# A recommender forward pass with word rows gathered by three engines: instructions recorded with the kernel's own semaphores, and more columns fetched row by row

## The chip, the cores and the metric

The kernel runs on one core of a Trainium2 chip. The metric is the device time in microseconds of one execution, as the median of several. The trace is that of one profiled execution, and its span goes from the core's first instruction to its last.

The engines are TensorE (PE, with PEld for its weight loads), VectorE (DVE), ScalarE (ACT), GpSimd (POOL) and SyncE (SP). A name with q (SPq, ACTq) is an engine's sequencer, which issues DMAs.

## The reference

For each of 16384 rows, 32 word indices pick rows of 300 floats out of a table of 50000, and their mean is taken. Three groups of 20 indices and four single ones do the same with small tables of 64 columns, each with one more column for the "wide" sum. The 748 features go through three layers with ReLU and a last one with a sigmoid.

```python
tok = word_emb[token_idx].mean(axis=1)          # (16384, 300) from 32 rows each
e1 = emb_mh1[mh1_idx].mean(axis=1)              # tables of 1000, 5000, 10000 rows
...
o4 = emb_oh4[oh4_idx]                           # tables of 100, 50, 20, 1000 rows
emb = jnp.concatenate([tok, e1, e2, e3, o1, o2, o3, o4], axis=1)
wide = (wide_mh1[mh1_idx].sum(axis=(1, 2)) + ... + wide_oh4[oh4_idx][:, 0])[:, None]
h = jax.nn.relu(emb @ W1 + b1)                  # 748 -> 1024
h = jax.nn.relu(h @ W2 + b2)                    # -> 512
h = jax.nn.relu(h @ W3 + b3)                    # -> 256
return jax.nn.sigmoid(h @ Wd + bd + wide)
```

## The kernel before

The rows are worked in 128 tiles of 128. A tile has 11 steps (`STEPS`), and the main loop runs over `n_steps` = 128 x 11 + 27 = 1435 steps. In one step the program writes the instructions of several pieces of work, each by its own pace:

- Words. `tokens` goes over the 32 word columns of a tile in 16 groups of two. One indirect DMA on POOL gathers 128 rows of 300 floats (one column) into `tok_rows`, which has six buffers of two columns. Three groups later (`TOK_LAG`) `add_up` adds them on DVE into `own`, a PSUM bank; the last add of a tile goes into the features `g`.
- Some columns come another way. `fetch` lets SP read column 31 of a tile row by row: `load_column` loads the 128 indices into one partition (`columns`), `column_offsets` turns them into byte offsets with two operations on DVE, and for each 32 rows a TENSOR_LOAD reads 32 offsets into registers, and 32 DMAs of 1200 bytes follow, each behind a MOVE of the register, into one of two buffers `fetched`. A column is spread over 16.5 steps (`FETCH_STEPS`), and those of 83 tiles (from tile 4, all with t % 3 not 0) go this way. `ScalarRows` lets ACT read column 30 of 26 tiles likewise, 8 offsets per TENSOR_LOAD, into `fetched_scalar`. ACT's rows go out wherever the running number of transfers reaches one of two places of eight, so one for each three of SP's.
- Small tables. `one_hots` compares indices with an iota on DVE (`hot`), ACT scales half of it, `counts` multiplies one-hot matrices on PE into `pc`, and ACT evicts these counts as `cnt` in FP8. `small_sums` multiplies `cnt` with the tables' terms into `pg` on PE, and DVE reduces that into `g`.
- The layers run on blocks of 3, 2 or 1 tiles, on PE with ACT's eviction, some matmuls in each step.

Order and waits: PE, DVE, ACT and SP execute in the order in which the program is written (`manual_schedule`), and the framework sets the waits from the tile pools. Every hardware transfer takes one of eight semaphores in turn (the lanes DMAHW0 to 7, six of them for SP and two for ACT while ACT's rows run) and waits for the lane's last transfer; each gather does the same with the lanes DMASW0 to 7. Where an instruction has more waits than fit, an event instruction of its own stands ahead of it.

Of the kernel before, what the change touches and what calls it, by code (L numbers as in the profile page):

```python
# [14 lines left out]
U8 = mybir.dt.uint8  # L15
AF = mybir.ActivationFunctionType
# [13 lines left out]
FETCH_STEPS = 16.5  # L30
FETCH_AHEAD = {1: 25.0, 2: 19.5}
# [4 lines left out]
SCALAR_LANES = (6, 7)  # L36
SCALAR_FROM = 12
SCALAR_RATE = 2.55
SCALAR_MARGIN = 5.0
SCALAR_LOADS = 8  # L40
SCALAR_WANTED, SCALAR_LEAST = 8, 2
# [41 lines left out]

@with_exitstack
def kernel(
# [24 lines left out]
    M1, M2, M3 = D1 // P, D2 // P, D3 // P  # L110

# [8 lines left out]
    tokp = ctx.enter_context(tc.tile_pool(name="tok", bufs=TOK_BUFS))  # L120
    const = ctx.enter_context(tc.tile_pool(name="const", bufs=1))
    idxp = ctx.enter_context(tc.tile_pool(name="idx", bufs=4))
    keyp = ctx.enter_context(tc.tile_pool(name="keys", bufs=1))
    scp = ctx.enter_context(tc.tile_pool(name="sc", bufs=2))
    ohp = ctx.enter_context(tc.tile_pool(name="onehot", bufs=HOT_BUFS))
    cp = ctx.enter_context(tc.tile_pool(name="counts", bufs=2))
    fp = ctx.enter_context(tc.tile_pool(name="fetched", bufs=2))
    fa = ctx.enter_context(tc.tile_pool(name="fetched_scalar", bufs=2))
    gp = ctx.enter_context(tc.tile_pool(name="g", bufs=3))
    wp = ctx.enter_context(tc.tile_pool(name="wide", bufs=2))  # L130
    xp = ctx.enter_context(tc.tile_pool(name="x", bufs=1))
    hp = ctx.enter_context(tc.tile_pool(name="h", bufs=1))
    ps_h = ctx.enter_context(tc.tile_pool(name="ps_h", bufs=2, space=bass.MemoryType.PSUM))
    ps_c = ctx.enter_context(tc.tile_pool(name="ps_c", bufs=2, space=bass.MemoryType.PSUM))
    ps_g = ctx.enter_context(tc.tile_pool(name="ps_g", bufs=1, space=bass.MemoryType.PSUM))
    ps_v = ctx.enter_context(tc.tile_pool(name="ps_v", bufs=1, space=bass.MemoryType.PSUM))

# [13 lines left out]
    NK = len(chunk_rows)  # L151
    N_EARLY = 3

    transfers = []
    scalar_row = []

    def hardware_dma(queue, **operands):

        dma = queue.dma_start(**operands)  # L161
        if transfers and transfers[-1][0] is not queue:
            tc.add_manual_dep(
                dma.ins,
                transfers[-1][1],
                mybir.DependencyInfo(mybir.DependencyClass.NoSync, mybir.DependencyReason.DATA),
                reason="the semaphores of transfers are taken in this order",
            )
        transfers.append((queue, dma.ins.name))

    def sync_dma(**operands):

        while len(transfers) % LANES in SCALAR_LANES and scalar_row and scalar_row[0]():
            pass
        hardware_dma(nc.sync, **operands)

    ident = const.tile([P, P], F32, name="ident")
    make_identity(nc, ident)
    ident_bf = const.tile([P, P], BF16, name="ident_bf")
# [3 lines left out]
    scale = const.tile([P, NK], F32, name="scale")  # L183
# [11 lines left out]
    own = ps_v.tile([P, 512], F32, name="own")  # L195
    tok_sum = own[:, 128 : 128 + TOK_D]
    iota_i = keyp.tile([P, n_h], I32, name="iota_i", tag="low")
    nc.gpsimd.iota(iota_i, pattern=[[1, n_h]], base=0, channel_multiplier=0)
    iota_s = keyp.tile([P, n_h], BF16, name="iota_s", tag="keys")
# [4 lines left out]
    first = const.tile([P, 1, N_SMALL], I32, name="first")  # L204
# [6 lines left out]
    terms = const.tile([P, n_h, 3 * ROW], BF16, name="terms")  # L211
    early_use = fa.tile([P, TOK_D], F32, name="fetched_scalar")
# [6 lines left out]
    def load_tables(part0, tag):  # L219
        raw = hp.tile([P, PART, ROW], F32, name="raw", tag=tag)  # L220
# [12 lines left out]
        return raw  # L233

    def convert_tables():
# [19 lines left out]
        def make(p, c):  # L255
# [5 lines left out]
            left = ps_h.tile([P, SPLIT, ROW], F32, name="left", tag="ph")[:, 0 : b - a, :]  # L261
# [13 lines left out]
    w1_sb = const.tile([P, NK, D1], F32, name="w1_sb")  # L275
    w2_sb = const.tile([P, M1, D2], F32, name="w2_sb")
    w3_sb = const.tile([P, M2, D3], F32, name="w3_sb")
    wd_sb = const.tile([P, M3], F32, name="wd_sb")
    b1_sb = const.tile([P, M1], F32, name="b1_sb")
    b2_sb = const.tile([P, M2], F32, name="b2_sb")  # L280
    b3_sb = const.tile([P, M3], F32, name="b3_sb")
    bd_sb = const.tile([1, 1], F32, name="bd_sb")
# [14 lines left out]
    def features(t):  # L297
        if t not in g_of:
            g_of[t] = gp.tile([P, G_COLS], F32, name="g")
# [21 lines left out]
    def tokens():  # L321

        under_way = []
        for n in range(n_all):
            if n < n_all - TOK_LAG:
                t, q = divmod(n, n_groups)
                it = token_indices[t // NSUB][:, t % NSUB, :].bitcast(U32)
                tok_rows = tokp.tile([P, TOK_GROUP * TOK_D], F32, name="tok_rows")
                rows = []
                for r in range(TOK_GROUP):  # L330
                    j = q * TOK_GROUP + r
                    if (t, j) in fetched:
                        rows.insert(0, fetched.pop((t, j)))
                        continue
                    assert j != N_TOK - 2 or t not in asked_tiles
                    rows.append(tok_rows[:, r * TOK_D : (r + 1) * TOK_D])
                    gather = nc.gpsimd.indirect_dma_start(  # L337
                        out=rows[-1],
                        out_offset=None,
                        in_=word,  # L340
                        in_offset=bass.IndirectOffsetOnAxis(ap=it[:, j : j + 1], axis=0),
                    )
                    tc.stamp_issue_order_token(gather.ins, "gathers")
# [5 lines left out]
    fetched, columns, asked_tiles = {}, {}, set()  # L349
    all_columns = const.tile([P, P], I32, name="columns")  # L350
    uses = {True: 0, False: 0}
    word_bytes = word.bitcast(U8).rearrange("n d -> (n d)").unsqueeze(0)

    def load_column(t, j, by_scalar):
# [4 lines left out]
        operands = dict(out=columns[t, j], in_=idx[t * P : (t + 1) * P, j : j + 1].rearrange("n o -> o n"))  # L359
        if by_scalar:  # L360
            hardware_dma(nc.scalar, **operands)
        else:
            sync_dma(**operands)
# [9 lines left out]
    def load_offsets(column, p0, n, engine):  # L373

        _, values = nc.values_load_multi_w_load_instructions(
            column[:, p0 : p0 + n],
            engines=[engine],
            min_val=0,
            max_val=(word.shape[0] - 1) * ROW_BYTES,
            skip_runtime_bounds_check_because="the indices are rows of the table",  # L380
        )
        return values

    def fetch(t):


        rows = fp.tile([P, TOK_D], F32, name="fetched").bitcast(U8)
        column = columns.pop((t, N_TOK - 1))
        for p0 in range(0, P, LOADS):
            for i, value in enumerate(load_offsets(column, p0, LOADS, mybir.EngineType.SP)):  # L390
                p = p0 + i
                sync_dma(out=rows[p : p + 1, :], in_=word_bytes[:, bass.ds(value, ROW_BYTES)])
                if p == P - 1:
                    fetched[t, N_TOK - 1] = rows.bitcast(F32)
                yield 1

    class ScalarRows:
# [3 lines left out]
        def __init__(self, summed_at, column_due):  # L401
            self.summed_at, self.column_due = summed_at, column_due
            self.step, self.t, self.next_t = 0, None, None
            self.row, self.values, self.loaded, self.issued = P, [], P, 0
            self.ready, self.starts, self.asked = set(), [], True

        def choose(self, rows_before):

            least = self.step + (rows_before + P) / SCALAR_RATE + SCALAR_MARGIN
            t = next((t for t in range(tiles_all) if self.summed_at(t) >= least), None)  # L410
            if t is None or t > tiles_all - 3:
                return None
            return t

        def load(self, free):

            if len(self.values) >= (SCALAR_WANTED if free else SCALAR_LEAST):
                return
            if self.loaded == P:
                if self.next_t not in self.ready:  # L420
                    return
                self.starts.append(self.next_t)
                self.column, self.loaded = columns.pop((self.next_t, N_TOK - 2)), 0
                self.next_t = None
            self.values += load_offsets(self.column, self.loaded, SCALAR_LOADS, mybir.EngineType.Activation)
            self.loaded += SCALAR_LOADS

        def __call__(self):

# [567 lines left out]
```

## Time and profile before

| | |
|---|---|
| median of three runs | 7411.62 us |
| lowest and highest | 7397.10, 7412.59 us |
| span of the profiled execution | 5019.3 us |
| own time of the profiled execution | not given; the median stands 2392.3 us above the span |
| granted TensorE clock, mean | 0.990 |
| busy in the span: PE, PEld, DVE, ACT, POOL | 4806.3, 3721.3, 3748.7, 2726.5, 3774.2 us |
| gathers on POOL | 3987, 946 ns each |
| row DMAs on SP, on ACT | 10624, 3328 |

The profile counts an instruction of an engine as busy from its start to its end. DMA-issuing instructions are not counted as busy on SP and ACT, so these queues have to be read from the lists by tile and from the timeline, where `fetched` is SP's rows and `fetched_scalar` ACT's. The time outside the span is in no view of the profile.

### The profile page before, as it was taken

The page shows a single profiled execution, that of the slowest core. Times are in us where ns is not written, and L with a number is a line of the kernel's source. Part 1 is how long each engine was busy: PE and PEld are TensorE (multiplying, and loading weights), DVE is VectorE, ACT ScalarE, POOL GpSimd, SP SyncE. Part 2 cuts the span into 40 slices and gives each one's busy share as a digit, 9 for nine tenths or more (in the row PEclk, how much of TensorE's full clock was granted, in tenths as well). Part 3 has the DMA queues.
Part 4 walks back from the last instruction along what each step waited for, and adds up shares of the span by engine and source line. Part 5 has one row for each costly group of instructions (what it writes and reads, how often), then busy time and mean ns, then how long its engine had stood idle before and what let it go on. Part 6 is the DMA issues. An engine that isn't in the chain of part 4 may idle for free.

```text
span 5019.3 us, 124363 instructions
## 1 busy us (share of the span) xinstructions
PE 4806.3 (96%) x36356; PEld 3721.3 (74%) x36356; DVE 3748.7 (75%) x6830; ACT 2726.5 (54%) x3658; POOL 3774.2 (75%) x3994
## 2 busy tenths in 40 slices
PE   6799999999999999999999999999999999999999
PEld 4577777777777777777777777667767888888899
DVE  6777777777777777777777777777777777777774
ACT  5455555555555555555555555555555555555552
POOL 7777777777777777777777777777777777777775
PEclk8899999999999999999999999999999999999999
DMA  7444444444444444444444444444444444444443
GB/s 204 127 129 130 129 129 129 129 130 129 129 130 128 129 130 129 130 129 129 129 129 129 130 129 129 130 129 129 130 130 129 129 129 130 130 129 130 129 128 100
DMA packets 291735, 654.13 MB, mean 130 GB/s; under 512 B 147100, under 2 KB 161692, under 8 KB 291048
## 3 DMA queue, kind: packets, MB, share of 16 engines
q0 software_dynamic: 191376, 612.66, 45.1%
q1 hardware_dynamic: 89271, 29.49, 2.7%
q10 hardware_dynamic: 10400, 4.02, 0.4%
q8 instruction: 284, 4.65, 0.4%
q14 instruction: 404, 3.30, 0.2%
HBM read 645.65 MB, written 0.07 MB: 129 GB/s over the span
## 4 chain that ended last, share of the span: by engine, by line
PE 37%; DMA 26%; DVE 15%; issue 12%; POOL 9%; ACT 1%; SPq 1%; ACTq 0%; DVEq 0%; POOLq 0%
DMA tok_rows<-in_word_emb_dram,it 23%; PE ph L677 17%; PE pg L554 14%; POOL tok_rows L337 9%; DVE hot L501 5%; DVE own L319 4%; PE pc L519 4%; DVE own L314 3%; DMA fetched_scalar<-in_word_emb_dram 1%; DMA fetched<-in_word_emb_dram 1%; PE pc L595 1%; DVE g L544 1%; PE po L719 1%; SPq L161 1%; DVE x L599 0%
## 5 line engine op out<-in xcount | busy, mean ns | idle before, releaser
L337 POOL DMA_INDIRECT tok_rows<-in_word_emb_dram,it x3987 | 3773.3, 946 | 1219.3 <-issue 754.1
L508 ACT ACTIVATE hot<-hot 64x768 bf16<-64x768 bf16 (+1 forms) x1408 | 1155.4, 821 | 1820.6 <-DVE hot L501 1664.0
L554 PE MATMUL pg<-terms,cnt 128*128 128x195 bf16 x17664 | 1723.7, 249 | 35.6 <-DVE g L544 35.0
L554 PEld LDWEIGHTS <-cnt 128*128 128x128 fp8e3 x17664 | 1529.2, 98 | 83.1 <-issue 54.4
L677 PE MATMUL ph<-x,w_sb 128*128 128x384 f32 (+5 forms) x4932 | 1473.8, 437 | 16.2 <-ACT h L688 11.9
L501 DVE TENSOR_TENSOR hot<-own,sc 128x1656 bf16<-128x1656 bf16 (+1 forms) x1408 | 1393.7, 990 | 126.7 <-PE pc L519 37.7
L522 ACT ACTIVATE cnt<-pc 128x828 uint16<-128x828 f32 (+1 forms) x1408 | 1186.5, 843 | 181.5 <-PE pc L519 103.2
L319 DVE TENSOR_TENSOR own<-own,tok_rows 128x300 f32<-128x300 f32 x1792 | 857.1, 478 | 513.3 <-DMA tok_rows<-in_word_emb_dram,it 468.5
L677 PE MATMUL ph<-h,w_sb 128*128 128x384 f32 (+2 forms) x4160 | 1225.9, 435 | 14.2 <-ACT h L688 14.0
L314 DVE TENSOR_TENSOR own<-own,tok_rows 128x300 f32<-128x300 f32 x1827 | 873.8, 478 | 271.9 <-DMA tok_rows<-in_word_emb_dram,it 221.0
L677 PEld LDWEIGHTS ph<-x,w_sb 128*128 128x128 f32 (+1 forms) x4932 | 830.8, 191 | 305.7 <-ACT h L688 23.0
L519 PEld LDWEIGHTS <-hot 128*128 128x128 bf16 x8192 | 594.2, 98 | 523.8 <-issue 271.3
L677 PEld LDWEIGHTS ph<-h,w_sb 128*128 128x128 f32 x4160 | 700.6, 191 | 266.1 <-ACT h L688 27.3
L519 PE MATMUL pc<-hot 128*128 128x138 bf16 x8192 | 733.1, 225 | 111.8 <-ACT hot L508 51.7
L688 ACT ACTIVATE h<-ph,b_sb 128x384 f32<-128x384 f32 (+2 forms) x723 | 378.7, 524 | 210.5 <-PE ph L677 115.4
L544 DVE TENSOR_REDUCE g<-pg 128x130 f32<-128x390 f32 (+1 forms) x512 | 259.2, 506 | 140.0 <-PE pg L554 138.7
L599 DVE TENSOR_TENSOR x<-pc,scale 128x768 f32<-128x768 f32 x127 | 120.8, 951 | 58.8 <-PE pc L595 57.5
L595 PE MATMUL pc<-ident,g 128*128 128x128 f32 x762 | 107.3, 278 | 5.7 <-ACT cnt L522 5.4
L312 DVE TENSOR_TENSOR own<-tok_rows 128x300 f32<-128x300 f32 x128 | 61.5, 481 | 55.3 <-DMA tok_rows<-in_word_emb_dram,it 52.6
L595 PEld LDWEIGHTS pc<-ident,g 128*128 128x128 f32 x762 | 83.7, 143 | 9.8 <-ACT cnt L522 9.3
L488 DVE COPY sc<-pc 128x512 bf16<-128x512 bf16 x64 | 44.0, 688 | 40.5 <-PE pc L484 39.8
L719 PE MATMUL po<-h,wd_sb 128*1 128x384 f32 (+2 forms) x208 | 67.4, 442 | 4.4 <-ACT h L688 4.4
(59 smaller groups left out, 514.6 us busy)
## 6 DMA issues: line engine op xcount, KB each, us to landing
fetched<-in_word_emb_dram SPq DMA_DIRECT2D x10624, 1.2 KB
tok_rows<-in_word_emb_dram,it POOLq DMA_INDIRECT x3987
fetched_scalar<-in_word_emb_dram ACTq DMA_DIRECT2D x3328, 1.2 KB
ix<-in_idx_dram SPq DMA_DIRECT2D x64, 64.0 KB
w_sb<-in_W_dram SPq DMA_DIRECT2D x6, 512.0 KB
raw<-in_mh_dram SPq DMA_DIRECT2D x4, 682.5 KB
it<-in_idx_dram SPq DMA_DIRECT2D x64, 32.0 KB
w_sb<-in_W_dram SPq DMA_DIRECT2D x1, 2048.0 KB
```

The lines of the kernel that those rows point to most:

```text
L314: nc.vector.tensor_add(tok_sum, tok_sum, a)
L319: nc.vector.tensor_add(to, tok_sum, b)
L337: gather = nc.gpsimd.indirect_dma_start(out=rows[-1], out_offset=None, in_=word, in_offset=bass.IndirectOffsetOnAxis(ap=it[:, j : j + 1], ...
L501: nc.vector.tensor_tensor(hot[:, 0 : 2 * rows, :].rearrange("p i (n d) -> p i n d", d=2), iota.rearrange("p (n d) -> p n d", d=2).unsqueez ...
L508: nc.scalar.activation(upper, upper, AF.Copy, scale=UPPER)
L519: nc.tensor.matmul(pc[:, k // n, at : at + n_h], hot[:, 2 * k, 0:P], hot[:, 2 * k + 1, :], start=True, stop=True)
L522: nc.scalar.activation(cnt[:, :, b : b + rows].rearrange("l h (g k) -> l h g k", g=2), pc[:, :, 0 : n * n_h].rearrange("l g (k h) -> l h g ...
L544: nc.vector.tensor_reduce(field_columns(features(t), pair), pg[:, 0:n, :].rearrange("p f (c d) -> p f d c", c=3), AX.X, ALU.add,)
L554: nc.tensor.matmul(pg[:, j, :], by_slice[:, h, :], terms[:, h, :], start=(h == h0), stop=(h == h1 - 1))
L595: nc.tensor.transpose(pt[:, j // n, j % n, :], g[:, c : c + P], ident)
L677: nc.tensor.matmul(to, weights[: src.shape[0], k, m * P : (m + 1) * P], src, start=(k == 0), stop=(k == len(srcs) - 1),)
L688: nc.scalar.activation(dst()[:, m, 0:n], ph[:, 0:n], AF.Relu, bias=bias[:, m : m + 1])
```

## The change

The framework's pools, schedule and waits are replaced by classes of the kernel's own. `Queue` and `Program.record` record each instruction with the regions that it reads and writes; from these follow its waits, without those that another wait already implies. `Program.emit` writes all recorded instructions at the end, in one critical section, in the recorded order on each engine, with the kernel's own semaphores: one for each engine that is waited for, eight lanes for other transfers, one for each of the six `tok_rows` buffers, and eight in turn for SP's columns and for ACT's. `Ring` and `Banks` are fixed buffers in place of pools.

A batch is the gathers of one `tok_rows` buffer, or the 128 rows of a column. Whoever reads one waits for its last member, and its members wait for nothing of their own:

```diff
+    def record(self, emit, sequencer, stream, reads, writes, clear=(), batch=None):
+        ins = Instruction(emit, sequencer, self.stream(stream))
+        if batch is not None:
+            batch.append(ins)
+            ins.batch = batch
+        needed = {}
+        def need(other):
+            other = other.batch[-1]
+            if other.batch is ins.batch:
+                return
...
+        waits = [o for s, o in needed.items() if known.get(s, 0) < o.tick]
+        waits = [
+            o
+            for o in waits
+            if not any(d is not o and d.knows(o.stream) >= o.tick for d in waits)
+        ]
...
-                    gather = nc.gpsimd.indirect_dma_start(
...
-                    tc.stamp_issue_order_token(gather.ins, "gathers")
+                    program.gather(f"gather{tokp.slot}", rows[-1], word, it[:, j : j + 1], batch, tok_rows)
```

The row fetches are planned anew. `RowFetches` sets column behind column from a first step, `FETCH_STEPS` or 128 / `SCALAR_RATE` steps each, and picks for each the next tile whose sum is wanted at least `FETCH_MARGIN` steps after its end. SP's first column starts at step 31 and its last ends at step 1423; DVE prepares a column's offsets one step before its rows start. ACT's rows no longer hang on the lanes: three are issued in each step ahead of `one_hots`, two behind it.

```diff
-FETCH_STEPS = 16.5
-FETCH_AHEAD = {1: 25.0, 2: 19.5}
+FETCH_STEPS = 14.5
+FETCH_MARGIN = 3.0
...
-SCALAR_LANES = (6, 7)
-SCALAR_FROM = 12
-SCALAR_RATE = 2.55
+ROW_SEMAPHORES = 8
+SCALAR_FROM = 8
+SCALAR_BEFORE, SCALAR_AFTER = 3, 2
+SCALAR_RATE = SCALAR_BEFORE + SCALAR_AFTER
...
+            by_sync.prepare(step)
+            by_scalar.prepare(step)
+            scalar_rows(step, SCALAR_BEFORE)
             if i < STEPS - 1:
                 hot = one_hots(sc, s, i + 1)
...
-            fetch_rows(step, 0.5)
+            scalar_rows(step, SCALAR_AFTER)
+            sync_rows.to(step + 0.5)
             flush_outputs()
             counts(cnt, hot_now, i)
-            fetch_rows(step, 1)
+            sync_rows.to(step + 1)
```

| in the program | before | after |
|---|---|---|
| columns fetched by SP, by ACT | 83, 26 | 96, 52 |
| row DMAs on SP, on ACT | 10624, 3328 | 12288, 6656 |
| TENSOR_LOADs on SP, on ACT | 332, 416 | 384, 832 |
| gathers on POOL | 3987 | 3948 |
| event instructions, all engines | 8164 | 3100 |
| of them on DVE, POOL, ACT, SP | 5487, 2032, 92, 529 | 1889, 52, 1096, 52 |

On PE the instructions and their order stay; of its waits before, 2171 stood on weight loads and 1579 on matmuls, and of the 2424 after, all stand on weight loads.

SP before, in the middle of a column: each row is one instruction with the wait for its lane, here with the block's indices (`it`, `ix`) between.

```order
L161 DMA fetched<-in_word_emb_dram 1x1200 [waits DMAHW0_49]
L161 DMA fetched<-in_word_emb_dram 1x1200 [waits DMAHW1_49]
L375 TENSOR_LOAD columns [waits DVE_49]
L161 DMA fetched<-in_word_emb_dram 1x1200 [waits DMAHW2_49,DVE_49]
L161 DMA fetched<-in_word_emb_dram 1x1200 [waits DMAHW3_49]
L161 DMA fetched<-in_word_emb_dram 1x1200 [waits DMAHW4_49]
L161 DMA fetched<-in_word_emb_dram 1x1200 [waits DMAHW5_49]
L161 DMA it<-in_idx_dram 128x2x32 [waits DMASW5_49,DMASW4_49,DMASW6_49,DMASW3_49,DMASW7_49,DMASW2_49,DMAHW0_49,DMASW1_49,DMASW0_49]
```

SP after, from the last rows of one column (`fetched_80`) into the next: rows without waits stand as one line with their count.

```order
L259 TENSOR_LOAD columns
L238 DMA fetched_80<-in_word_emb_dram 1x1200 x32
L259 TENSOR_LOAD columns [waits sem_DVE]
L238 DMA fetched_81<-in_word_emb_dram 1x1200 x32
L259 TENSOR_LOAD columns
L238 DMA fetched_81<-in_word_emb_dram 1x1200 x32
L259 TENSOR_LOAD columns
L238 DMA fetched_81<-in_word_emb_dram 1x1200 x19
L232 DMA out_dram<-x 3x1x128 [waits sem_ACT]
```

A column's rows have no wait any more; its first load of offsets waits for DVE's two operations, and the store of results, which stands between rows, for ACT.

ACT before, in the steady part: one or two rows between its ACTIVATEs, each with its lane.

```order
L161 DMA fetched_scalar<-in_word_emb_dram 1x1200 [waits DMAHW7_49]
L522 ACTIVATE cnt<-pc 128x138x6 [waits PE_49]
L508 ACTIVATE hot<-hot 64x6x128 [waits DVE_49]
L688 ACTIVATE h_39476<-ph,b_sb 128x384 [waits PE_49]
L522 ACTIVATE cnt<-pc 128x138x6 [waits PE_49]
L161 DMA fetched_scalar<-in_word_emb_dram 1x1200 [waits DMAHW6_49]
```

ACT after, in the same part: three rows ahead of the scaling of `hot`, two behind it.

```order
L238 DMA fetched_scalar_82<-in_word_emb_dram 1x1200 x3
L112 ACTIVATE hot_77<-hot_77 64x6x128 [waits sem_DVE]
L238 DMA fetched_scalar_82<-in_word_emb_dram 1x1200 x2
L112 ACTIVATE cnt_78<-pc_94 128x138x6 [waits sem_ACT,sem_PE]
L238 DMA fetched_scalar_82<-in_word_emb_dram 1x1200 x3
L112 ACTIVATE hot_76<-hot_76 64x6x128 [waits sem_DVE]
L259 TENSOR_LOAD columns
```

Every step now has its five rows, without waits, and the load of the next eight offsets stands among them.

DVE before: each add waits for its own gather.

```order
L314 TENSOR_TENSOR own<-own,tok_rows 128x300 [waits DMASW5_49,DVE_49]
L319 TENSOR_TENSOR own<-own,tok_rows 128x300 [waits DMASW6_49,DVE_49]
L314 TENSOR_TENSOR own<-own,tok_rows 128x300 [waits DMASW7_49,DVE_49]
L319 TENSOR_TENSOR own<-own,tok_rows 128x300 [waits DMASW0_49,DVE_49]
L501 TENSOR_TENSOR hot<-own,sc 128x1104 [waits DVE_49,PE_49,Activation_49]
```

DVE after: the first add of a pair waits for the buffer's semaphore, so for both gathers, and the second for the first add.

```order
L112 TENSOR_TENSOR hot_77<-own,sc_74 128x1656 [waits sem_PE]
L112 TENSOR_TENSOR own<-own,tok_rows_65 128x300 [waits sem_gather4,sem_DVE]
L112 TENSOR_TENSOR own<-own,tok_rows_65 128x300 [waits sem_DVE]
L112 TENSOR_REDUCE g_84<-pg 128x65 [waits sem_PE]
L112 TENSOR_REDUCE wide_87<-g_84 128x1 [waits sem_DVE]
L112 TENSOR_TENSOR g_84<-wide_87,g_84 128x1 [waits sem_DVE]
```

Where a pair's add waited for one transfer, it now waits for the later of two.

More of the change, by code (lines that the diff above doesn't have):

```diff
@@ new lines, in size_of, with on_chip, __init__, next @@
+def size_of(tensor):
+    n = 1
+    for d in list(tensor.shape)[1:]:
+        n *= int(d)
+    return n * SIZES[tensor.dtype]
+def on_chip(ap):
+    return ap.space in (bass.MemoryType.SB, bass.MemoryType.PSUM)
+class Banks:
+    def __init__(self, program, pool, shape, name, bufs):
+        self.program = program
+        self.free = [
+            pool.tile(shape, F32, name=f"{name}{k}", tag=f"{name}{k}") for k in range(bufs)
+        ]
+    def next(self):
+        if not self.free:
+            self.flush()
+        bank = self.free.pop(0)
+        self.program.taken[bank.tensor.name] = (self, bank)
+        return bank
@@ L84, with __init__, next, slot @@
+class Ring:
+    def __init__(self, pool, shape, dtype, name, bufs):
+        self.all = [
+            pool.tile(shape, dtype, name=f"{name}{k}", tag=f"{name}{k}") for k in range(bufs)
+        ]
+        self.used = 0
+    def next(self):
+        self.used += 1
+        return self.all[(self.used - 1) % len(self.all)]
+    @property
+    def slot(self):
+        return (self.used - 1) % len(self.all)
 @with_exitstack
@@ L150 @@
     chunk_at = [1, 1 + 2 * ROW, 1 + 4 * ROW, WIDE_AT, G_COLS - 2 * P, G_COLS - P]
-    NK = len(chunk_rows)
     N_EARLY = 3
[L154 to L169, printed above, removed]
     def sync_dma(**operands):
[L173 to L177, printed above, removed]
+        return program.dma(core.sync, **operands)
+    ident = tile_of([P, P], F32, "ident")
     make_identity(nc, ident)
-    ident_bf = const.tile([P, P], BF16, name="ident_bf")
+    ident_bf = tile_of([P, P], BF16, "ident_bf")
     nc.vector.tensor_copy(ident_bf, ident)
-    scale = const.tile([P, NK], F32, name="scale")
+    scale = tile_of([P, NK], F32, "scale")
     nc.vector.memset(scale, 1.0)
@@ L358, in load_column @@
         columns[t, j] = all_columns[at : at + 1, :]
[L359 to L363, printed above, removed]
+        asked.add((t, j))
+        program.dma(
+            core.scalar if by_scalar else core.sync,
+            out=columns[t, j],
+            in_=idx[t * P : (t + 1) * P, j : j + 1].rearrange("n o -> o n"),
+        )
     def column_offsets(t, j):
@@ L371, in column_offsets, with fetch @@
         nc.vector.tensor_single_scalar(column, column, low.bit_length() - 1, op=ALU.logical_shift_left)
[L373 to L392, printed above, removed]
+    def fetch(t, j, by_scalar, loads):
+        queue, ring = (core.scalar, fa) if by_scalar else (core.sync, fp)
+        tile_rows = ring.next()
+        rows = tile_rows.bitcast(U8)
+        lane = f"{'ACT' if by_scalar else 'SP'}rows{rings[by_scalar] % ROW_SEMAPHORES}"
+        rings[by_scalar] += 1
+        column, batch = columns.pop((t, j)), []
+        for p0 in range(0, P, loads):
+            values = program.load(queue, column[:, p0 : p0 + loads], last_offset)
+            yield 0
+            for p in range(p0, p0 + loads):
+                program.row(queue, lane, rows[p : p + 1, :], lambda values=values: values.pop(0), word_bytes, batch)
@@ L393, in fetch @@
                 if p == P - 1:
[L394 removed]
+                    fetched[t, j] = tile_rows
                 yield 1
[L397 to L417, printed above, removed]
[L418 to L449 removed]
@@ L451, in load_indices, with __init__, to @@
+    class Paced_rows:
+        def __init__(self, fetches, steps):
+            self.fetches, self.steps, self.done = fetches, steps, 0
+        def to(self, now):
+            if not self.fetches.due:
+                return
+            target = P * (now - self.fetches.due[0][0]) / self.steps
+            while self.done < target and self.fetches.one(now):
+                self.done += 1
     def load_indices(blk):
         b0 = blk * BLOCK
-        it = idxp.tile([P, NSUB, N_TOK], I32, name="it")
+        it = idxp.next()
@@ L497, in one_hots @@
         rows = min(ONEHOT, HALF - b)
[L498 removed]
+        hot = ohp.next()
         shape = [P, 2 * rows, n_h // 2, 2]
@@ L880 @@
                     sc = next_sc
-                cnt = cp.tile([P, n_h, HALF], U16, name="cnt", tag="counts")
+                cnt = cp.next()
         if t < tiles:
@@ L957 @@
     flush_stores(True)
+    program.emit([program.members[program.stream(f"lane{k}")][-1] for k in range(LANES)])
 def kernel(**inputs):
```

412 lines of the change are left out of this document (295 added, 117 removed).

## The prediction

> **What bounds the kernel now.** I read the page's first rows, then the groups by line, the waits, the timeline around the engine that never rests, and last the DMA queues of SyncE and ScalarE.
>
> ```profile
> span 5019.3 us, 124363 instructions
> PE 4806.3 (96%) x36356; PEld 3721.3 (74%) x36356; DVE 3748.7 (75%) x6830; ACT 2726.5 (54%) x3658; POOL 3774.2 (75%) x3994
> L337 POOL DMA_INDIRECT tok_rows<-in_word_emb_dram,it x3987 | 3773.3, 946 | 1219.3 <-issue 754.1
> ```
>
> PE looks like the limit at 96% and POOL idle for a quarter. The timeline of POOL says otherwise:
>
> ```profile
> 2.84 1.10 POOL L337 DMA_INDIRECT tok_rows<-in_word_emb_dram,it  x1 [1.36 <-DMA it<-in_idx_dram]
> 4.25 0.95 POOL L337 DMA_INDIRECT tok_rows<-in_word_emb_dram,it  x1 [0.30 <-issue]
> 5.50 0.94 POOL L337 DMA_INDIRECT tok_rows<-in_word_emb_dram,it  x1 [0.30 <-issue]
> ...
> 2499.72 0.95 POOL L337 DMA_INDIRECT tok_rows<-in_word_emb_dram,it  x1 [0.30 <-issue]
> 2500.97 0.96 POOL L337 DMA_INDIRECT tok_rows<-in_word_emb_dram,it  x1 [0.30 <-DVE ix L470]
> 2502.23 0.95 POOL L337 DMA_INDIRECT tok_rows<-in_word_emb_dram,it  x1 [0.30 <-issue]
> ...
> 4993.07 0.95 POOL L337 DMA_INDIRECT tok_rows<-in_word_emb_dram,it  x1 [0.30 <-DVE own L319]
> ```
>
> The first number is the start, the second the length, the bracket the idle time ahead. A gather starts every 1.25 us, at 4.25 us, when its buffers are free, as in the middle, whatever name stands behind the arrow: 0.30 is a fixed gap, not a wait. From the first start to the last, 4993.07 - 2.84 = 4990.2 us are 3986 periods of 1.252 us, so nearly no gather ever waited. GpSimd's issue of gathers is the floor. DVE shows it from the other side, waiting for gathers for 689 us in the two largest of its waits:
>
> ```profile
> DVE own L319 <- DMA tok_rows<-in_word_emb_dram,it: 468.5, 683, 2.8
> DVE own L314 <- DMA tok_rows<-in_word_emb_dram,it: 221.0, 333, 3.1
> ```
>
> After the last gather starts, 5019.3 - 4993.07 = 26.2 us of tail remain. PE is close behind, but it has idle time and is fed at POOL's pace.
>
> The span is 5019.3 us and the median of the runs 7411.62 (7397.10 to 7412.59). The 2392.3 us between them lie outside the trace. I sum against the span and hold these 2392.3 us constant, which no row can confirm. A change under 0.2%, some 15 us, can't be told from none here.
>
> **The gathers.** Columns fetched row by row go from 83 + 26 = 109 to 96 + 52 = 148, so 39 gathers go, 3987 to 3948. At 1.252 us each: -48.8 us, span 4970.5, time 7362.8. That is the whole gain on offer, and GpSimd's floor is also why the removed waits of the gathers are worth nothing: the gathers of 2.84 to 5.50 us, which wait for no buffer, come no faster. Bounds for the period without waits: 0.95 us (no gap) to 1.252; I take 1.252, since the early gathers have it.
>
> The adds now wait for both gathers of a pair at once, so a pair's first add (0.48 us) no longer runs before the second lands. There are about 1900 pairs, so DVE loses 0 to 1900 x 0.478 = 908 us of cover; its idle time is 5019 - 3749 = 1270 us. I take 0: DVE would still fit, and six buffers of two columns leave POOL 15 us before it needs a buffer again. If that cover went, POOL would wait for DVE, which shows as more than 0.30 ahead of a gather.
>
> **SyncE's rows.** This queue decides the case.
>
> ```profile
> L161 SPq MOVE fetched<-in_word_emb_dram x10624: 29/29/39, 114.2 to 4966.1; - x197
> L161 SPq DMA_DIRECT2D fetched<-in_word_emb_dram x10624: 217/225/604, 114.3 to 4966.2; - x197
> L375 SPq TENSOR_LOAD <-columns x332: 2025/2127/2373, 112.1 to 4953.7; - x166
> L161 SPq DMA_DIRECT2D columns<-in_idx_dram x83: 537/557/601, 76.0 to 4897.9; - x83
> L161 SPq DMA_DIRECT2D ix<-in_idx_dram x64: 590/610/1009, 1.3 to 4749.4; - x64
> L161 SPq DMA_DIRECT2D it<-in_idx_dram x64: 410/423/3307, 0.8 to 4748.9; - x64
> L161 SPq DMA_DIRECT2D out_dram<-x x52: 217/795/841, 314.0 to 5017.2; - x52
> ```
>
> Its work after: 384 loads of offsets x 2.127 = 817 us, 96 columns x 0.557 = 53, 64 x 0.610 = 39, 64 x 0.423 = 27, 52 x 0.795 = 41, and, as an estimate, 0.045 for the gap ahead of each of these 660 = 30: 1007 us besides the rows. The rows are 96 x 128 = 12288 of r us each. The first column starts at step 31, which is here:
>
> ```profile
> 146.01 0.87 ACT L522 ACTIVATE cnt<-pc 128x828 uint16<-128x828 f32 x1
> 4855.20 9.96 SPq L161 DMA_DIRECT2D fetched<-in_word_emb_dram  x32
> 1828.78 10.54 SPq L161 DMA_DIRECT2D fetched<-in_word_emb_dram  x32
> SPq L161 <- DMA fetched<-in_word_emb_dram: 132.3, 541, 0.6
> ```
>
> The columns stand one behind the other, so from there SyncE has no spare step, and DVE, which prepares each next column's offsets in its own order, can't run over three steps ahead of it. A span paced by SyncE is thus 146 + 1007 + 12288 r + the tail of 26 = 1179 + 12288 r. It meets GpSimd's 4970.5 at r = 0.3085, and the span of before at 0.3125.
>
> What is r? A row is a MOVE and a DMA, 0.029 + 0.217 to 0.225, and two gaps. No row of before goes without a wait for its transfer lane; after, only a column's first rows wait. Bounds: from below DMA and MOVE without any gap, 0.246; from above a middling stretch of before, (10.54 - 0.225)/31 = 0.333. Between them stands the best stretch of before, (9.96 - 0.225)/31 = 0.314, in which no lane was late though each was looked at. It is the nearest row: after, each lane's lateness (132 us as the waits name it) is gone, and the look at it too. Of its 0.060 us in gaps I let that look take 0.009 and take r = 0.305; this is a choice, and 0.006 would be enough to reach 0.3085. Then SyncE needs 1179 + 3748 = 4927 us, 43 us less than GpSimd, and the removed lane waits and the added 1664 rows both cost nothing in the sum; what hides them is the gathers' period. If r stays at 0.314 that cover is gone: 5037 us, 18 more than before.
>
> [...]
>
> **ScalarE's rows.**
>
> ```profile
> L161 ACTq DMA_DIRECT2D fetched_scalar<-in_word_emb_dram x3328: 213/214/746, 309.9 to 4790.8; - x196
> L375 ACTq TENSOR_LOAD <-columns x416: 716/763/1013, 307.0 to 4770.6; - x139
> ACT hot L508 <- DMA fetched_scalar<-in_word_emb_dram: 95.1, 92, 3.0
> ACT h L688 <- DMA fetched_scalar<-in_word_emb_dram: 62.9, 84, 1.7
> ACT cnt L522 <- DMA fetched_scalar<-in_word_emb_dram: 49.8, 67, 1.6
> ...
> 2000.23 0.84 ACT L508 ACTIVATE hot<-hot 64x768 bf16<-64x768 bf16 x1 [2.19 <-DVE hot L501]
> 2000.31 0.77 ACTq L161 DMA_DIRECT2D fetched_scalar<-in_word_emb_dram  x2
> ACT hot L508 <- DVE hot L501: 1664.0, 1089, 5.0
> ```
>
> Rows go from 3328 to 6656, five in a step: three ahead of the scaling of `hot`, two ahead of the eviction of `cnt`, for which PE and DVE wait. Issue after: 6656 x 0.303 (0.214, MOVE 0.029, gaps estimated at the 0.060 of SyncE's) + 832 x 0.763 = 2652 us. The lane waits of 208 us go. The row at 2000.31 is issued while the ACTIVATE of 2000.23 runs, so issue lies beside work: bounds 0 (all beside it) and 2652 + 2726 = 5378 us for ScalarE (none). I take 0: 408 us of the 2652 beside work are enough to stay under 4970, and the 1664 us that it waits for DVE have room.
>
> **PE's waits, DVE's event instructions.** The order on PE is kept, but 1579 waits that stood on a matmul now stand on the weight load ahead of it, so that load can't be drawn ahead. Bounds: 0, and 1579 x 98 ns (next row) = 155 us. 4806 + 155 = 4961 still lies under 4970. I take 0; what hides it is the wait for POOL.
>
> ```profile
> L554 PEld LDWEIGHTS <-cnt 128*128 128x128 fp8e3 x17664 | 1529.2, 98 | 83.1 <-issue 54.4
> ```
>
> The waiting instructions that go from DVE (some 3600) and POOL (2000) lie on no path that sets the end, as DVE waits for gathers; 0, at best some of DVE's 1270 us of slack. SP and ACT each carry rows behind their few remaining waits (a result store waits for ScalarE), a fraction of a column's slack of three steps. The sum: -48.8 us, 7362.8, say 7363.
>
> **The rivals.**
> - SyncE paces, slower: rows stay at 0.314 or above. For it: no stretch of 32 in the trace is shorter, and the middling one has 0.333. Against: all of them carry lanes. It decides from r = 0.3138 on: 0.314 gives 5037 (7430), 0.326 gives 5185 (7577), 0.333 gives 5271 (7663). Its own range is 7428 to 7580.
> - A balance: r of 0.311 to 0.314 puts the span at 5001 to 5037, or PE's lost draw-ahead eats the gain: 7393 to 7427.
> - ScalarE becomes the bound: rows three ahead of `hot` arrive late at PE in each step. If under 408 us of its issue lie beside work, the span goes to 4970 and beyond, up to 5378 (7770). Against it: the overlap at 2000.31.
> - Rows exclude each other. On ScalarE the median of 214 stands at the minimum of 213 while SyncE issues beside it, so most rows of the two do not hold each other up. [...]
> - The time outside the span grows with the program, some 5% longer: 2392 x 0.05 = +120 us, 7482. No row speaks to it.
>
> **How the numbers follow.** GpSimd paces: 0.45, as 0.3085 lies 0.006 below a measured stretch with looks in it. Balance 0.14. SyncE paces 0.31. ScalarE 0.04, exclusion 0.02, the time outside 0.04. The first alone is faster by over 0.2%, the second the same, the rest slower: 0.45, 0.14, 0.41. The likeliest gives 7363, in its own range 7340 (the gap of the runs, 15 us, and a period of 1.247) to 7396. Over it the range must reach into SyncE's case up to r = 0.325, 5173 or 7565; what is left out above is its upper end, ScalarE, exclusion, about 0.12, and 0.03 below 7340.
>
> **What would show it.** Right: 3948 gathers at 1.25 us with 0.30 ahead of each, a span near 4970, SyncE's stretches of 32 rows under 9.8 us, no wait of DVE or POOL for SyncE. Wrong by SyncE: stretches of 10 us or more, gathers with over 0.30 idle ahead, SyncE without idle time, DVE waiting for `columns`. Wrong by ScalarE: PE waiting for `hot` or `cnt` in each step. Wrong outside: a shorter span, and a time that doesn't follow.

## The result and the profile after

The changed kernel took 7680.4 us (7660.6 to 7711.9) where the kernel before took 7405.9: a ratio of 1.0365 [1.0331, 1.0400], slower. The forecast was 7363, faster, with a range up to 7565.

One thing has to be known before these numbers can be read. The trace of before that the forecast used has a span of 5019 us, and its times of 7400 us were measured where the kernel before runs 1.46 to 1.48 times as long. The experiments met both kinds: on four chips the kernel before takes 5021 to 5032 us, on a fifth 7329. I speak of two kinds of chips, since each set of runs was on one chip and the runs of a set agree; whether it is the chip, or something else that was under way on it, no run shows. A run's time lies 1.8 us above its span on either kind (7711.94 against 7710.2, 5020.65 against 5018.9), so nothing like 2392 us lies outside a span. I read the change first on the chips of 5021 us, since there the two traces can be set side by side. The changed kernel's own repeat there (e5 below) takes 5265.3 us, ratio 1.0487 [1.0471, 1.0503].

The page of that repeat, its span, its engines and the chain that ended last:

```profile
span 5262.9 us, 129842 instructions
PE 4880.6 (93%) x36356; PEld 3767.5 (72%) x36356; DVE 3636.4 (69%) x6908; ACT 2732.6 (52%) x3658; POOL 3739.0 (71%) x3955
SPq 42%; PE 27%; issue 12%; DVE 7%; DMA 6%; POOL 2%; ACT 2%; ACTq 1%; DVEq 0%
```

The same part of the page of before, which was not shown yet:

```profile
PE 37%; DMA 26%; DVE 15%; issue 12%; POOL 9%; ACT 1%; SPq 1%; ACTq 0%; DVEq 0%; POOLq 0%
```

SPq had 1% of the chain before and has 42% now, more than any other engine. The groups on POOL and of the offsets' operations on DVE (count, busy time, mean, idle time before and its releasers), and the waits:

```profile
L244 POOL DMA_INDIRECT tok_rows<-in_word_emb_dram,it x3948 | 3738.1, 947 | 1494.7 <-issue 909.9 <-DVE own L112 464.4 <-DVE hot L112 54.5
L112 DVE TENSOR_SCALAR columns<-columns 1x128 int32<-1x128 int32 x296 | 72.6, 245 | 412.4 <-DMA columns<-in_idx_dram 405.7
...
DVE columns L112 <- DMA columns<-in_idx_dram: 405.7, 79, 10.4
DVE own L112 <- DMA tok_rows<-in_word_emb_dram,it: 118.0, 109, 4.3
```

The 39 gathers went, but GpSimd's idle time rose from 1219 to 1495 us. DVE stands 406 us before `columns`, a transfer that lies in SyncE's queue behind rows. It isn't the transfer that is slow, but SyncE that comes to it late: DVE starts on a column 2.8 us (median) after SyncE issues its transfer, where in the trace of before it came to it 11.7 us after. For gathers DVE waits 118 us, where it was 689; its adds free the buffers late, so POOL waits for DVE. SyncE's rows themselves, by tile (shortest, median, longest in ns; first and last start):

```profile
L238 SPq MOVE fetched<-in_word_emb_dram x12288: 29/29/39, 145.2 to 5206.7; - x199
L238 SPq DMA_DIRECT2D fetched<-in_word_emb_dram x12288: 217/225/705, 145.3 to 5206.7; - x199
L259 SPq TENSOR_LOAD <-columns x384: 2029/2132/2384, 143.1 to 5194.1; - x192
```

From 145.3 to 5206.7 us SyncE is at work without a pause: the longest gap between two of its instructions is 1.6 us. Two stretches of 32 rows from its timeline, one of the best and one near the median:

```profile
3118.04 9.91 SPq L238 DMA_DIRECT2D fetched<-in_word_emb_dram  x32
3380.40 10.37 SPq L238 DMA_DIRECT2D fetched<-in_word_emb_dram  x32
```

That is (9.91 - 0.225)/31 = 0.312 and 0.327 us a row, against 0.314 and 0.333 of the two stretches of before. Without the lanes' waits the best stretch is 2 ns shorter.

On the chip of the result the same kernel shows this (span, engines and the chain; a group of POOL; rows of SyncE):

```profile
span 7710.2 us, 129842 instructions
PE 5706.7 (74%) x36356; PEld 4144.7 (54%) x36356; DVE 3628.6 (47%) x6908; ACT 2735.0 (35%) x3658; POOL 3747.9 (49%) x3955
SPq 35%; issue 25%; PE 19%; DVE 8%; another core or an unknown queue 8%; ACT 2%; DMA 1%; ACTq 1%; DVEq 0%
...
L244 POOL DMA_INDIRECT tok_rows<-in_word_emb_dram,it x3948 | 3747.0, 949 | 3911.8 <-DVE own L112 2612.0 <-issue 966.1 <-DVE g L112 271.3
...
L238 SPq MOVE fetched<-in_word_emb_dram x12288: 1/29/1565, 201.1 to 7619.7; - x199
L238 SPq DMA_DIRECT2D fetched<-in_word_emb_dram x12288: 2/219/1476, 201.2 to 7620.0; - x199
3926.48 6.48 SPq L238 DMA_DIRECT2D fetched<-in_word_emb_dram  x6
```

A gather takes 949 ns as ever, but a MOVE of a register, 29 ns at the median, takes up to 1565, and six rows take 6.48 us. SyncE's queue has the largest share of the chain there too, and its rows go on from 201 to 7620 us.

The starts in this trace show when it is slow. From the start of a row's MOVE to the next one's, a row takes 0.679 us in the mean within 1.26 us of a gather's start (6450 rows), and 0.334 where no gather has started for 4 us (2201 rows). In e9, e10 and e11 below it is 0.663 to 0.674 and 0.330 to 0.331. So SyncE runs at half speed beside gathers there and at its usual one without them. In the trace of e5, rows within 1.26 us of a gather's start take 0.330.

### The profile page after: what moved, and what is told of

Same layout as the page of the kernel before. It is cut to its first block, busy times and chain, and to the rows that moved or that the text cites. A ratio compares the mean times of both kernels' runs of the same rounds, so it can differ in the third digit from the quotient of the medians.

```text
span 7710.2 us, 129842 instructions
## 1 busy us (share of the span) xinstructions
PE 5706.7 (74%) x36356; PEld 4144.7 (54%) x36356; DVE 3628.6 (47%) x6908; ACT 2735.0 (35%) x3658; POOL 3747.9 (49%) x3955
## 4 chain that ended last, share of the span: by engine, by line
SPq 35%; issue 25%; PE 19%; DVE 8%; another core or an unknown queue 8%; ACT 2%; DMA 1%; ACTq 1%; DVEq 0%
SPq L238 29%; PE ph L112 10%; PE pg L112 7%; SPq L259 5%; DVE own L112 3%; DVE hot L112 3%; PE pc L112 3%; DMA columns<-in_idx_dram 1%; SPq L232 1%; ACTq L238 1%; DVE g L112 1%; ACT hot L112 1%; ACT cnt L112 0%; DVE columns L112 0%
## 5 line engine op out<-in xcount | busy, mean ns | idle before, releaser
L112 PE MATMUL pg<-terms,cnt 128*128 128x195 bf16 x17664 | 2097.0, 271 | 814.2 <-issue 598.6
L112 PEld LDWEIGHTS pg<-terms,cnt 128*128 128x128 fp8e3 x17664 | 1711.1, 107 | 1044.7 <-issue 743.3
L112 PE MATMUL ph<-x,w_sb 128*128 128x384 f32 (+5 forms) x4932 | 1670.7, 479 | 155.9 <-issue 91.2
L112 PEld LDWEIGHTS pc<-hot 128*128 128x128 bf16 x8192 | 643.4, 105 | 1172.4 <-ACT hot L112 553.8
L112 PE MATMUL ph<-odd,w_sb 128*128 128x384 f32 (+2 forms) x3328 | 1110.8, 473 | 108.7 <-issue 66.7
L112 PEld LDWEIGHTS ph<-odd,w_sb 128*128 128x128 f32 x3328 | 617.6, 210 | 365.6 <-issue 149.9
L112 ACT ACTIVATE odd<-ph,b_sb 128x384 f32<-128x384 f32 (+2 forms) x515 | 270.3, 525 | 451.7 <-remote 216.4
L112 PE MATMUL ph<-even,w_sb 128*128 128x384 f32 (+2 forms) x832 | 285.4, 479 | 73.5 <-ACT even L112 50.5
L112 PEld LDWEIGHTS ph<-even,w_sb 128*128 128x128 f32 x832 | 156.3, 210 | 147.5 <-ACT even L112 58.2
L112 ACT ACTIVATE even<-ph,b_sb 128x384 f32<-128x384 f32 (+2 forms) x208 | 108.7, 524 | 229.3 <-remote 146.9
```

The source lines that it names most:

```text
L112: lambda: call(*args, **operands), self.name, self.name, aps + list(named.values()), outs
```

## The experiments

Each is compared with the kernel before on its own chip; "before" is given where it isn't 5021 us.

**e1, the kernel before, repeated.** 

> The kernel before, unchanged, with a trace of its own. In the trace of the changed kernel SyncE's instructions stall in steps of about 0.71 us, 4290 of them with 3024 us in sum, nearly all while GpSimd issues gathers back to back; the trace of before that the forecast used has 22 such steps. Theory S (SyncE's stalls set both times, and that trace was of an execution without them): the span is near the time, 7390 to 7410 us, SyncE is never idle, with over 2000 us in steps of 0.7 us, and gathers stand idle for over 2000 us. Theory O (2392 us of the kernel before lie outside the span, and the change's loss is a new one of its own): the span is 5019 us again at a time of 7400.

Measured: 5020.9 us, span 5018.9, ratio 0.9999 [0.9989, 1.0009], 21 steps of 0.7 us on SyncE. Neither theory as I put it: the kernel is the same and its span is that of the first trace, but its time is 2391 us shorter than the 7411.6 us on record. There is nothing to look for outside the span.

**e2, the recorded program with about the old counts.**

```diff
-FETCH_STEPS = 14.5
+FETCH_STEPS = 16.5
-SCALAR_BEFORE, SCALAR_AFTER = 3, 2
+SCALAR_BEFORE, SCALAR_AFTER = 2, 1
```

> The recorded program with about the old number of fetched columns: FETCH_STEPS 16.5 and two plus one ScalarE rows in a step, so 84 columns by SyncE and 31 by ScalarE, 3981 gathers. Theory S (SyncE paces, with a column costing 77 us as in the changed kernel): 84 x 77.3 + 230 = 6720 us. A variant of S, in which the stall goes with the gathers and not with the rows: about 7400, as before. Theory W (the new waits and the recorded order cost, whatever the counts): 7680 or more.

Measured: 5021.5 us, ratio 1.0000 [0.9991, 1.0010]; the numbers expected were for the other kind of chip. With 3981 gathers GpSimd's floor, the period of a gather with 33 us around all of them, is 3981 x 1.252 + 33 = 5017 us. So the recorded instructions, the batches' waits, the weight loads that wait now and the pairs' adds together gain nothing and cost 8 us at most (six gathers fewer than before, 7.5 us by their period, and 0.7 us more time): theory W falls, and the loss is in the counts.

**e3, no rows by SyncE or ScalarE.** (`RowFetches` with no tiles for either.) 

> The recorded program in which neither SyncE nor ScalarE fetches columns: 4096 gathers. Theory S: GpSimd paces, 4096 x 1.252 + 33 = 5160 us, with 0.30 us ahead of each gather. Theory W, or one in which the memory or the gathers themselves are slow in these executions: over 7000 us.

Measured: 5157.7 us, ratio 1.0272 [1.0251, 1.0292]. GpSimd's period and the tail give the time to 3 us.

**e4, the changed kernel without ScalarE's rows.** 

> The changed kernel without ScalarE's rows: 96 columns by SyncE, 4000 gathers. Theory S with stalls that come from gathers: SyncE still paces, 7400 to 7700 us. Theory X (SyncE's rows stall on ScalarE's rows): GpSimd paces, 4000 x 1.252 + 33 = 5041 us, or SyncE at 1179 + 12288 x 0.314 = 5037.

Measured: 5238.3 us, ratio 1.0432 [1.0411, 1.0453]. SyncE paces, without any row on ScalarE, and on a chip without the steps of 0.71 us. Theory X falls with its two numbers: 5041 and 5037 are both missed by 200 us, so a row of 0.314 us isn't what SyncE needs.

**e5, the changed kernel, repeated.** 

> The changed kernel, unchanged, on the chip on which the kernel before takes 5021 us. Theory S (SyncE's rows pace; without ScalarE's rows its 96 columns took 5236 us): 5236 to 5290 us, SyncE never idle, stretches of 32 rows of 10.0 us and more, DVE waiting some 400 us for columns. Theory P (the forecast: GpSimd paces): 4971 us. Theory C (ScalarE's rows stall SyncE's, whatever the chip): 5400 us or more.

Measured: 5265.3 us, as theory S has it; the lines are above. Against e4, which ran on another chip of this kind, ScalarE's 6656 rows add 27 us.

**e6, FETCH_STEPS 15.4.**

```diff
-FETCH_STEPS = 14.5
+FETCH_STEPS = 15.4
```

> The changed kernel with FETCH_STEPS 15.4: 90 columns by SyncE, 52 by ScalarE, 3954 gathers. Theory S: six columns fewer take 6 x (128 x 0.324 + 8.7 + 2) = 313 us from SyncE, 4923 to 4980, so GpSimd paces again: 3954 x 1.252 + 33 = 4983 us, 0.7% under the kernel before. Theory W (the new waits or ScalarE's rows cost by themselves): over 5021.

Measured: 4991.1 us, ratio 0.9940 [0.9927, 0.9954]: 0.6% under the kernel before, a small gain but clear of the runs' scatter, and 5% under the changed one. Six columns fewer on SyncE take off 274 us, although six more gathers are made. The chain, and POOL and the rows:

```profile
span 4989.5 us, 128257 instructions
PE 42%; POOL 17%; DMA 17%; DVE 12%; issue 8%; ACTq 2%; ACT 1%; SPq 1%; DVEq 0%; POOLq 0%
L244 POOL DMA_INDIRECT tok_rows<-in_word_emb_dram,it x3954 | 3744.2, 947 | 1215.7 <-issue 913.7 <-DVE own L112 198.0 <-DVE hot L112 74.1
L238 SPq DMA_DIRECT2D fetched<-in_word_emb_dram x11520: 213/224/598, 141.5 to 4899.0; - x199
DVE own L112 <- DMA tok_rows<-in_word_emb_dram,it: 856.4, 892, 4.0
```

SPq is back at 1% of the chain, POOL's idle time is 3954 gaps of 0.30 and little more, and DVE waits for gathers again. SyncE ends its rows at 4899 us, in time, but it has little room: its longest gap between 141 and 4899 us is 3.7 us, and a column takes it 4758/90 = 52.9 us (in e5 5061/96 = 52.7). In the span of 4989.5 us a step takes 3.48 us, so the plan allows a column 53.5 us with 15.4 steps, and 50.4 with 14.5.

**e7, no rows by SyncE.** 

> The changed kernel without SyncE's rows: 52 columns by ScalarE alone, 4044 gathers. If ScalarE's five rows in each step cost nothing, GpSimd paces: 4044 x 1.252 + 33 = 5096 us. If they hold PE up (theory A), over 5130.

Measured: 5100.4 us, ratio 1.0158 [1.0139, 1.0176]. Five rows a step on ScalarE are hidden, to 4 us of the 5096 expected.

**e8, 15.4 steps and six rows a step on ScalarE.** 

> As the one with 15.4 steps, with six ScalarE rows in a step (three ahead of one_hots, three behind) in place of five: 62 columns by ScalarE, 90 by SyncE, 3944 gathers. If ScalarE's rows stay hidden: 3944 x 1.252 + 33 = 4971 us. If ScalarE or its overlap with SyncE becomes the bound: 5000 or more.

Measured: 5002.9 us, ratio 0.9964 [0.9950, 0.9978]. Ten gathers fewer, and 12 us more than e6. DVE waits 79 us for `columns` again, so SyncE is late at times with ScalarE's added rows; its rows take 4768 us from first to last, 10 more than in e6. What else holds the kernel 32 us over the expected 4971 was not taken apart.

**e9 to e11** ran on a chip on which the kernel before takes 7328.9 us. e9 gives each of SyncE's rows its wait back, six lanes, at 15.4 steps:

```diff
+        if name == "SP":
+            self.row_lanes = getattr(self, "row_lanes", -1) + 1
+            lane = f"rowlane{self.row_lanes % 6}"
+            return self.record(emit, name, lane, [], [out], self.members[self.stream(lane)][-1:])
```

> As the one with 15.4 steps (90 columns, 4991 us), but each of SyncE's rows waits again for the last transfer on one of six lanes, as before. It gives the price of the waits that the change took away. Theory S: what the lanes' lateness cost a row in the kernel before, 0.350 less 0.325 us, comes back, 11520 x 0.025 = 288 us on the 4947 us that SyncE needs there: 5235 us. The step of the forecast (the look at a lane costs 0.009 us in each row): 11520 x 0.009 = 104 more, 5340. If the waits were worth nothing: 4991.

e10 gives each gather a semaphore of its own:

```diff
-program.gather(f"gather{tokp.slot}", rows[-1], word, it[:, j : j + 1], batch, tok_rows)
+program.gather(f"gather{tokp.slot}_{r}", rows[-1], word, it[:, j : j + 1], [], rows[-1])
```

> As the one with 15.4 steps, but each gather has a semaphore of its own, so the first add of a pair waits for its own gather alone. The forecast put the wait for both at 0: 4985 to 4997 us. If the pair's wait costs a late add in each pair that reaches GpSimd: under 4980.

e11 sets FETCH_STEPS to 14.9. 

> The changed kernel with FETCH_STEPS 14.9: 93 columns by SyncE, between the 90 that take 4991 us and the 96 that take 5265. Theory S (from the knee on, a column costs SyncE's 52.7 us): 5265 - 3 x 52.7 = 5107 us. If something sets in at once with the schedule of 14.5 steps instead, about 4990.

Measured: e9 7401.0 us, 1.0086 [1.0062, 1.0110]; e10 7358.9 us, 1.0033 [1.0020, 1.0045]; e11 7489.7 us, 1.0212 [1.0184, 1.0241]. Against the numbers expected, all three are inconclusive. Among themselves they say two things for such a chip: the rows' waits cost 42 us there (e9 against e10, if the gathers' semaphores cost nothing), and three more columns on SyncE cost 131 us (e11 against e10, on the same condition), 44 each. SyncE is late there with 90 columns already (DVE waits 405 us for `columns` in e10), so three more are a loss; what fewer than 90 would do, no run shows.

**e14, the changed kernel without its gathers** (the buffers are zeroed once and 3948 gathers are left out, so the gathered columns are missing in the result; the adds stay).

```diff
-program.gather(f"gather{tokp.slot}", rows[-1], word, it[:, j : j + 1], batch, tok_rows)
+if tokp.used <= TOK_BUFS:
+    nc.vector.memset(rows[-1], 0.0)
```

> The changed kernel without its 3948 gathers (the buffers are set to zero once; the sums of those columns are left out), 96 columns by SyncE and 52 by ScalarE. Theory S and G: SyncE paces at its own rows and nothing stalls it, 1179 + 12288 x 0.33 = 5235 us, on either kind of chip; somewhat less, down to 5040, if the gathers lengthen SyncE's rows. Rival (SyncE's stalls don't come from the gathers): 7000 or more where before takes 7300. Theory P (GpSimd paces): PE alone, under 4850.

Measured: 5235.8 us on a chip where before takes 5032.4, and 5238.5 on another. This is the plainest of the runs: with all of GpSimd's gathers gone the kernel takes the 5235 us that the sum for SyncE says, and stays within 0.6% of its time with the gathers. That the sum is met to 1 us is in part luck: the rows begin at 124 and not 146 us, and the tail behind them is 51 and not 26.

```profile
span 5236.6 us, 124167 instructions
SPq 45%; PE 31%; issue 11%; DVE 7%; DMA 3%; ACT 2%; ACTq 1%; DVEq 0%
L238 SPq DMA_DIRECT2D fetched<-in_word_emb_dram x12288: 217/224/865, 124.1 to 5185.3; - x199
DVE columns L112 <- DMA columns<-in_idx_dram: 443.9, 83, 10.9
```

The rows still take 5061 us from first to last, as with the gathers beside them. The gathers don't lengthen them on such a chip.

**e15, FETCH_STEPS 29**, 48 columns on SyncE. 

> The changed kernel with FETCH_STEPS 29: 48 columns by SyncE, 52 by ScalarE, 3996 gathers. Where before takes 5021: GpSimd paces, 3996 x 1.252 + 33 = 5036 us. Where it takes 7300, theory G with the rate that the runs there give (SyncE at 48% of its speed while gathers are issued, full speed else): 48 x 52.7 = 2530 us of work, of which 0.48 x 5003 fit beside the gathers, 130 remain, 5170 us. Rival (those chips are slower by a factor): 7300.

Measured: 5054.0 us where before takes 5032.4, ratio 1.0046 [1.0026, 1.0065]. The repeat of e7 on that chip (e13) stands 14 us above its first time, so the 18 us over 5036 are mostly the chip's. Where GpSimd paces, SyncE's columns save a gather's 1.25 us each and cost nothing: e15 stands 60 us under e13, with 48 gathers fewer.

**e12, e13, and repeats of e14, e7 and before (e16 to e18)** ask what SyncE does on chips of 7300 us. 

> The kernel before, unchanged, again with a trace. Theory G (where the kernel before takes 7300 to 7400 us, SyncE stalls in 0.71 us steps while GpSimd issues gathers, in this kernel too): near 7300 to 7400 with over 2000 us of such steps on SyncE, or 5021 with some 20 steps, according to the chip. Rival: a time of 7300 or more without such steps, so that something else sets it.

 

> The changed kernel without SyncE's rows, 4044 gathers. It took 5100 us where before takes 5021. Theory G (SyncE alone stalls, and GpSimd and ScalarE run as ever): 5100 us on a chip on which before takes 7300 too. Rival (all row fetches, or the gathers, are slow there): 6000 or more.

Measured: on their chips the kernel before takes 5032 and 5029 us. They gave 5032.7 and 5023.3 for the kernel before, 5114.3 and 5103.6 without SyncE's rows, and the 5238.5 without gathers that is told at e14. They repeat what stands above and leave the question of the other kind of chip open.

## Why the prediction was wrong, point by point

- **The step that failed is r, a SyncE row's time.** I took 0.305 us, from a best stretch of 0.314 less 0.009 for the look at a lane. On the chips of 5021 us the runs put 0.330 in its place: in e5 the rows run from 145.3 to 5206.7 us; the loads of offsets and the other transfers between take 1002 of these 5061 us (by the starts of neighbouring instructions), which leaves 4059/12288 = 0.330. On the chip of the result it is 0.53 us, with the steps told below. Two errors are in it. The look costs 1 to 2 ns and not 9: the gap ahead of a row's DMA is 30 ns at the median in the trace of before and 29 in e5, and the best stretch is 2 ns a row shorter. And the best stretch isn't the rows' mean: the rows of before that no lane held up took about 0.325 us in the mean, and the two stretches of e5 show the same spread. The stretch of 10.54 us that I called middling was a fast one, too: of the 171 whole stretches of 32 rows in the trace of before the median is 11.04 us, 0.349 a row with the lanes' lateness. The choice put r on the good side of the break-even of 0.3085 on the strength of 6 ns that no row showed.
- **The sum around it held.** With 0.330 it gives 1179 + 12288 x 0.330 = 5234; measured 5263 of span. The other 1007 us of SyncE's work were 1002 (the gap ahead of each of its 660 other instructions, estimated at 0.045 us, is 0.030 to 0.040 at the median in the trace of before), the first row came at 145 and not 146; the tail was 56 and not 26 us. The rival "SyncE paces" named the mechanism, the point of decision and the signs (DVE waiting for `columns`, SyncE without idle time), with 5185 us for 0.326 and 5271 for 0.333. Its range in time, 7428 to 7580, was missed by 100 us as well, since neither its row of 0.33 us nor the 2392 us on top of it hold on the chip of the result.
- **GpSimd's floor held** to 8 us wherever it paced on the chips of 5021 us (e2, e3, e6, e7): 1.252 us a gather and 33 around. Taking 39 gathers away was worth 49 us only with SyncE within it, and e6 shows it: 30 us faster with 33 gathers fewer, of 41 by the floor.
- **The terms put at 0 held:** the pairs' wait, the event instructions and PE's weight loads (together, in e2), ScalarE's five rows (e7, 4 us over the floor). One more that the sum left at 0 is small: ScalarE's 6656 rows cost a SyncE row 1.7 ns (0.3286 in e4, 0.3303 in e5), 21 us of the 27 by which e5 is longer. The rival in which rows exclude each other shows at most in these 1.7 ns.
- **The 2392 us "outside the span" was a misreading.** It was the difference between a trace from one kind of chip and times from the other. I said that no row could confirm that it stays constant, and then added it as one. The forecast's range, and the share of a gain in it, hung on a base that its trace didn't show. The other way round, the loss of 244 us on the chips of 5021 would have been 5265 + 2392 = 7657 by that sum, near the 7680 measured, by chance: on the result's chip a row takes 0.53 us and not 0.33.

## What to carry to other kernels

Before a queue is given more work, add up all that it must issue, by the mean and not the best of its rows, and set it against the bound of today: here 1007 + 12288 x 0.325 = 5001 us of SyncE work, by the mean of the unhindered rows (without its start and its tail), stood against a floor of 4970, and taking the waits away could not mend that. The semaphore waits that were already satisfied when SyncE reached them gave back 1 to 2 ns of a row's 330 here (the gap ahead of its DMA, 30 ns before and 29 in e5; the best stretches, 0.314 and 0.312 us a row). And if a trace's span and the measured times are far apart, ask whether they are of the same execution before anything is put "outside".

## What the runs showed of the hardware that I had not expected

- The kernel before takes 1.46 times as long and more on some chips (7328.9 and 7405.9 us against 5021), but not every instruction is slower there: a gather of the changed kernel takes 949 ns there and 947 in e5. The granted TensorE clock is lower there, 0.863 to 0.867 in the runs of the result against 0.968 in e5. SyncE's instructions, MOVEs included, stall there in steps of about 0.71 us: 4290 intervals of 0.68 to 0.78 us in the changed kernel's trace, 3024 us in sum, against 22 in the trace of before. They go with the gathers: while its rows go out, 4109 of them begin within 2 us of a gather's start (5263 us of the trace), 175 between 2 and 4 us after one (1121 us), and 3 later than that (1035 us). The traces of e9, e10 and e11 show the same, with 0 to 2 later than 4 us. PE loses time in the changed kernel's trace with nothing to wait for that the profile shows, too:

```profile
PEld pg L112 <- issue: 743.3, 785, 6.7
PE pg L112 <- issue: 598.6, 701, 6.5
PEld ph L112 <- issue: 502.9, 881, 17.6
```

  What stalls them, why on these chips alone, and whether the kernel before stalls alike there, stays open: that the steps go with the gathers is seen in four traces, but no run of those chips lacks the gathers, and none has a trace of the kernel before.
- On the chips of 5021 us a SyncE row (MOVE and DMA with an offset from a register) costs 0.33 us of its queue, whether or not 128-row gathers run beside it: 5061 us for 96 columns in e5 and in e14 alike.
